# Attention block with a local convolution: key buffers of the last group, order of the first query stack, place of the local norms, and fetch of the softmax sums

## The chip, the cores and the metric

The kernel runs on one core of one Trainium2 chip. The metric is the device time of one execution in microseconds (us). The engines are named as in the profile: PE (TensorE, matrix products; PEld its weight loads), DVE (VectorE), ACT (ScalarE), POOL (GpSimd) and SP (SyncE, which here issues transfers only). Each works off its own instructions in the order in which the program gives them and waits for others by semaphores.

## The reference

For four images of 384 channels and 48 x 48 pixels (2304 tokens), in float32, eight heads of 48 channels:

```python
local = lax.conv_general_dilated(x, conv_w, window_strides=(1, 1), padding='SAME', feature_group_count=C)   # 7 x 7, one filter a channel
local = local * inv[None, :, None, None] + (bn_beta - bn_mean * inv)[None, :, None, None]
x_norm = _layernorm(x_flat, ln_gamma, ln_beta)
q, k, v = heads(x_norm @ qkv_w.T + qkv_b)
local_q = heads(_layernorm(local_flat, ln_gamma, ln_beta))
q = q + local_q
attn = softmax(einsum('bhnd,bhmd->bhnm', q, k) * scale)
out = einsum('bhnm,bhmd->bhnd', attn, v) @ proj_w.T + proj_b
out = x_flat + out
```

(`heads` stands for the reshape to eight heads; the rest is cut.)

## The kernel before

**Tiling.** Keys, values and projections go by six token groups of 384 columns (g = 0 to 5; `G`). Queries go by five groups of rows (8, 10, 10, 10, 10 rows: 384 or 480 columns), numbered t = 0 to 19 over the four images, so that t = 0, 5, 10, 15 begin an image. Heads are worked in four pairs.

**Stages.** First a prologue makes image 0's keys, values and queries group by group (the loop `for g in range(1, NG)` from L1063). Then, for each t, twelve slots follow: slot s takes head pair s // 3 and six of the eighteen key blocks of 128 tokens. In a slot `score_batch` has PE compute six blocks of scores (36 matmuls, L952), ACT takes the exponential of each block from PSUM into a `pt` buffer (L960), and `weigh_batch` has PE multiply the six blocks into the values (24 matmuls, L967) and ACT copy the sums out (L849, L859). Before t = 5, 10 and 15 stands a key stage (`"kv"`, L1112 and on) which makes the next image's keys and values and also projects and writes out the image before.

**PSUM.** All products use pairs of banks from one rotation of four (`two_banks`, L105): scores, sums, means, projections. A product whose pair is still to be read stops PE, and everything behind it.

**The convolution** runs on DVE: 147 taps (49 for each of three channel chunks) for each t, one instruction a tap (L305, L309), into `acc{t}`, which rotates through three buffers. A planner (`plan`, L398) spreads the taps over half slots and steps of the key stage, in proportion to the room that `spare` and `spare_at_keys` (L336, L364) say DVE has there, so that each `acc{t}` is done at its due point; `convolve("slot", t, s, half)` issues the taps of one point. In image 0's prologue `convolve_first(n)` issues fixed numbers.

**The local norm** of `acc{t+1}` (class `Norm`, L419) takes, in image 0, the means over channels with PE: a sum over chunks on DVE (`sum`, L451-452), the mean on PE (`mean_of_sum`, L478), `centre` on DVE (L489), squares on ACT (L446), their sum on DVE (`sum_squares`, L451-452 again) and mean on PE, `root` on ACT (Ln, Exp, Square: L497-499), `newton` on DVE (L505-506), then `local_end` (L797) and `query_end` (L806), which adds the result to the projected queries. These steps hang on slot numbers counted from `first`, 8 for t = 0 and 7 for t = 1 to 3; `early` is true for t = 0 to 3 of image 0 only. Later images move the sums over partitions through DRAM (`out`, `few_...`).

**The query stack** of a pair, `qs`, holds the high part (`high_queries`, ACT, L820), the low part (`low_queries`, DVE, L825) and copies of rows moved by six SP transfers (L830, L832). The first score of t waits for the stack of pair 0.

**The keys.** Projection u of group g gives a tile `k` in the rotation `pt` of four, high part by ACT (L658), low part by DVE (`low`, L661, called by `lows_out`). `keys_out` then issues the transfers that lay them out: for u = 0 on SP straight into the stack of pair 0 (`ks`, L591-594), for the others on POOL into DRAM (`wide`, L591-619). POOL also loads the later stacks (`load_keys`, L628) and the slabs of x.

**The sums.** `divide(t)` fetches the softmax sums from DRAM with an SP transfer (`rd`, L888), takes reciprocals on DVE (L889) and spreads them (`rb`). In the key stage it is called at group 1 (L1140). SP takes its transfers in order; one that waits holds those behind it.

Of the kernel before, what the change touches and what calls it, by code (L numbers as in the profile page):

```python
# [16 lines left out]
P = 128  # L17
NH = 8
# [29 lines left out]
def unshifted_pass(  # L48
# [287 lines left out]
    def spare(t, s, half):  # L336
        b, g = divmod(t, NA)
        first, second = norm_slots(t)
        time = 3.6 - (0.0 if half else 0.6) - (0.6 if half and s % 3 == 1 else 0.0)
        if b + 1 < B and g >= begins(b + 1):  # L340
            time -= {(2, 1): 2.3, (4, 1): 2.2, (5, 1): 2.3, (7, 0): 0.4, (8, 0): 2.6}.get(
                (s, half), 0.0
            )
        if g:
            time -= {(2, 0): 0.7, (7, 1): 1.4}.get((s, half), 0.0)
        if t + 1 < NA:
            time -= {(first + 1, 0): 1.4, (first + 2, 0): 4.3, (first + 3, 0): 0.6}.get(
                (s, half), 0.0
            )
        elif g < NA - 1:  # L350
            time -= {(3, 1): 2.3, (5, 1): 2.2, (6, 1): 2.3, (8, 0): 0.4, (9, 0): 4.5}.get(
                (s, half), 0.0
            )
        return max(0.3, time) * columns_of(t) / G
# [64 lines left out]
    class Norm:  # L419
# [73 lines left out]
        def root(self, at=None):  # L493
            at = slice(0, self.n) if at is None else at

            y, u = self.buf[:, 1, at], self.buf[:, 2, at]
            nc.scalar.activation(u, self.m[:, at], AF.Ln, bias=eps)  # L497
            nc.scalar.activation(y, u, AF.Exp, scale=-0.5)
            nc.scalar.activation(u, y, AF.Square, scale=0.5**0.5)

        def newton(self, at=None):
            at = slice(0, self.n) if at is None else at
# [127 lines left out]
    def from_x(b, g, before=None, ao=None):  # L630
# [22 lines left out]
        def key(u, r):  # L653
            project(r[:, :G], lambda c: w_qk[:, c, 1, u, :], lambda c: src[:, c, :])
            yield
            bias = qkb[:, 1, u : u + 1]
            k = work.tile([P, 2, GM], HALF, tag="pt", name=f"k{b}_{g}_{u}", bufs=4)[:, :, :G]
            nc.scalar.activation(k[:, 0, :], r[:, :G], AF.Identity, bias=bias)  # L658

            def low():  # L660
                nc.vector.scalar_tensor_tensor(  # L661
                    k[:, 1, :], r[:, :G], bias, k[:, 0, :], ALU.add, ALU.subtract
                )
                keys_out(b, g, u, k)

            lows.append(low)
            yield
# [210 lines left out]
                        out=ao[r + HD : r + 64, c, :], in_=ao3[r + 16 * c : r + 16 * c + 16]  # L878
                    )

    def divide(t):

        n = columns_of(t)
        few = NH * n // P
        rd = work.tile([P, NH * GM // P], F32, tag="rd", name="rd")[:, :few]
        rb = work.tile([P, CC, GM], F32, tag="rb", name="rb", bufs=1)[:, :, :n]
        rden = dram.tile([NH, n], F32, tag=f"rden{n}", name=f"rden{t}")
        nc.sync.dma_start(out=rd, in_=outputs[t][2].rearrange("h (k f) -> (h k) f", f=few))  # L888
        nc.vector.reciprocal(rd, rd)  # L889

        for bound, op in ((SAFE, ALU.is_le), (1 / SAFE, ALU.is_ge)):
# [47 lines left out]


    halves = [slice(64 * i, 64 * i + 64) for i in range(2)]
    jobs = deque()
    weighing = deque()

    def score(t, p, kb):
# [29 lines left out]
    def score_batch(t, s):  # L975
        p, k0 = s // (KB // BATCH), s % (KB // BATCH) * BATCH
        for kb in range(k0, k0 + BATCH):
            score(t, p, kb)

    def weigh_batch(t, s):  # L980
        p, i = s // (KB // BATCH), s % (KB // BATCH)
# [81 lines left out]
    for g in range(1, NG):  # L1063

        last = g == NG - 1
        making = from_x(0, g)
        both(making)
        assert not last or n_first >= each - PE_TAPS
        norm = Norm(accs[0] if last else xn[0, g + 1])
        norm.mean_by_chunk(norm.src)  # L1070
        if last:
            added = output_bias()
        if g in (3, 5):
            keep_stack(0, g // 2 - 1)
        convolve_first(8 if last else 7)
        norm.centre()
        norm.squares()
        both(making)
        if not last:
            convolve_first(6)  # L1080
            both(making)
        norm.mean_by_chunk(norm.buf)
        norm.root()
        if last:
            convolve_first(9)
        lows_out(1)
        if last:
            both(making)
        both(making)
        convolve_first(4 if last else 9)  # L1090
        if not last:
            lows_out(2)
        if last:
            local_end(0, norm.newton())
        else:
            norm.scale(norm.newton())
        next(making)
        if last:
            query_end(0)
            high_queries(0, 0)  # L1100
            low_queries(0, 0)
        next(making)
        if not last:
            convolve_first(7)
    lows_out(2)
    nc.vector.tensor_add(pb, pb, added)
    plan(n_first - (each - PE_TAPS))
# [2 lines left out]
    for t in range(NT):  # L1110
        b, g = divmod(t, NA)
        if g == 0 and b:  # L1112
# [4 lines left out]
            for gk in range(NG):  # L1117
# [6 lines left out]
                old = norms_x.get(gk - 1)  # L1124
                both(making)
                convolve("kv", t, gk, 0)
                if new is not None:
                    norms_x[gk] = Norm(xn[b, new])
                    norms_x[gk].sum()
                    norms_x[gk].out()  # L1130
# [6 lines left out]
                    old.few_variance()  # L1137
                    old.few_root()
                if gk == 1:
                    rb = divide(t - 1)  # L1140
                if gk == 5:
                    norm.few_variance()
                    norm.few_root()
# [7 lines left out]
                    high_queries(t, 0)  # L1151
                both(making)
                convolve("kv", t, gk, 2)
                lows_out(1)
                if new is not None:
                    norms_x[gk].few_centre()
                    norms_x[gk].squares()
                if gk == 4:
                    norm.few_centre()
                    norm.squares()  # L1160
                if gk == 5:
                    low_queries(t, 0)
                both(making)
                convolve("kv", t, gk, 3)
                lows_out(2)
# [17 lines left out]
        first, second = norm_slots(t)  # L1183
        for s in range(NSLOT):
            pair, part = divmod(s, KB // BATCH)
            if t == 0 and s == first + 3:
                high_queries(t + 1, 0)
            score_batch(t, s)
            if part == 0 and pair < NP - 1:
                high_queries(t, pair + 1)  # L1190
# [32 lines left out]
                norm_x.few_variance()  # L1223
            if following and s == second:
                norm.few_variance()
            if t == 0 and s == first + 3:
                low_queries(t + 1, 0)
            convolve("slot", t, s, 0)
            sums_add()
            if early and s == first:  # L1230
# [2 lines left out]
            if early and s == first + 1:  # L1233
                norm.centre()
                jobs.extend(norm.square_jobs())
            if early and s == first + (2 if t == 0 else 3):
                local_end(t + 1, norm.newton())
                query_end(t + 1)
            if coming and s == X_SLOTS[1]:
                norm_x.few_root()  # L1240
            if following and s == second:
                norm.few_root()
            weigh_batch(t, s)
            if early and s == first:
                norm.mean_of_sum()
            if t == 0 and s == first + 1:
                norm.mean_kept(norm.buf)
                norm.root()
            if t and early and s == first + 2:
                norm.mean_of_sum()  # L1250
                norm.root()
            if t and early and s == first + 3:
                high_queries(t + 1, 0)
            convolve("slot", t, s, 1)
            if part == 0 and pair < NP - 1:
                low_queries(t, pair + 1)
            if t and early and s == first + 1:
                norm.sum_squares()
            if t and early and s == first + 3:
                low_queries(t + 1, 0)  # L1260
            if following and s == second + 1:
                low_queries(t + 1, 0)
            if coming and s == X_SLOTS[0]:
# [580 lines left out]
```

## Time and profile before

| | us |
|---|---|
| median of 3 runs (2768.09 to 2769.07) | 2768.7 |
| profiled execution | 2768.89 |
| its span, first to last instruction | 2767.1 |
| idle of PE in the span (2767.1 - 2728.2) | 38.9 |
| one slot of 384 columns: scores 3.42, weighing 4.09, from one slot's start to the next | 7.38 |
| one slot of 480 columns: scores 4.17, weighing 5.05, from start to start | 9.08 |
| one tap on DVE, mean over all | 0.66 |
| one exponential on ACT, mean | 0.94 |

The granted TensorE clock was 0.996 on average. In lines of the profile an arrow `<-` stands between what is written and what is read; `x6` is a number of instructions; in timelines the first two numbers are the start and the length in us, and brackets hold the idle time of the engine before it and what ended it. `SPq` marks a transfer's issue by SyncE. In the list of waits the numbers are the total in us, how often, and the longest; in tables by stretches each engine has its busy time with the number of instructions, and after POOL come the granted clock, the share of the transfer engines, and GB/s.

### The profile page before, as it was taken

The page shows a single profiled execution, that of the slowest core. Times are in us where ns is not written, and L with a number is a line of the kernel's source. Part 1 is how long each engine was busy: PE and PEld are TensorE (multiplying, and loading weights), DVE is VectorE, ACT ScalarE, POOL GpSimd, SP SyncE. Part 2 cuts the span into 40 slices and gives each one's busy share as a digit, 9 for nine tenths or more (in the row PEclk, how much of TensorE's full clock was granted, in tenths as well). Part 3 has the DMA queues.
Part 4 walks back from the last instruction along what each step waited for, and adds up shares of the span by engine and source line. Part 5 has one row for each costly group of instructions (what it writes and reads, how often), then busy time and mean ns, then how long its engine had stood idle before and what let it go on. Part 6 is the DMA issues. An engine that isn't in the chain of part 4 may idle for free.

```text
span 2767.1 us, 46151 instructions
## 1 busy us (share of the span) xinstructions
PE 2728.2 (99%) x16374; PEld 1547.9 (56%) x16374; DVE 2354.3 (85%) x4114; ACT 1638.4 (59%) x2262; POOL 695.0 (25%) x1273
## 2 busy tenths in 40 slices
PE   9999999999999999999999999999999999999999
PEld 6565555555555655555555665555555565555555
DVE  7999999999898999989889899898788899986202
ACT  4356666676324766776622666767652276666662
POOL 5741101112375111010257310101126711110110
PEclk9999999999999999999999999999999999999999
DMA  7454544446356455454545554545635545444442
GB/s 141 97 141 124 130 121 123 125 133 182 87 152 156 116 147 129 123 146 120 158 129 143 159 143 120 131 131 140 148 109 159 145 128 133 138 135 128 145 146 72
DMA packets 163297, 369.14 MB, mean 133 GB/s; under 512 B 61488, under 2 KB 112208, under 8 KB 163056
## 3 DMA queue, kind: packets, MB, share of 16 engines
q0 software_dynamic: 76992, 284.75, 36.0%
q1 hardware_dynamic: 83072, 77.72, 12.5%
q10 hardware_dynamic: 2992, 3.62, 0.4%
q8 instruction: 132, 2.16, 0.3%
q14 instruction: 109, 0.89, 0.1%
HBM read 258.14 MB, written 64.14 MB: 116 GB/s over the span
## 4 chain that ended last, share of the span: by engine, by line
PE 83%; DVE 6%; DMA 5%; POOL 3%; issue 1%; SPq 1%; ACT 1%; DVEq 0%; ACTq 0%; POOLq 0%
PE o L967 40%; PE r L952 33%; PE r L568 9%; DVE acc L309 3%; DMA wide<-k 1%; POOL wide L594 1%; DMA qs<-qs 1%; DMA slab<-in_x_dram 1%; POOL wide L619 1%; DMA parts<-part 1%; DVE k L661 0%; POOL wide L592 0%; DVE xn L806 0%; DVE acc L797 0%; POOL wide L613 0%
## 5 line engine op out<-in xcount | busy, mean ns | idle before, releaser
L309 DVE SCALAR_TENSOR_TENSOR acc<-slab,vec,acc 128x470 f32<-128x470 f32 (+9 forms) x2871 | 1687.7, 662 | 1.2
L960 ACT ACTIVATE pt<-r 128x960 f32<-128x960 f32 (+1 forms) x1440 | 1249.2, 943 | 272.7 <-PE o L967 151.4
L967 PE MATMUL o<-pt,v 128*64 128x480 f32 (+1 forms) x5760 | 1166.2, 554 | 4.6 <-ACT pt L960 4.6
L952 PE MATMUL r<-qs,ks 64*128 64x480 f32 (+1 forms) x8640 | 976.7, 375 | 19.2 <-DMA qs<-qs 13.3
L952 PEld LDWEIGHTS r<-qs,ks 64*128 64x128 f32 x8640 | 790.6, 185 | 286.6 <-issue 178.1
L967 PEld LDWEIGHTS o<-pt,v 128*64 128x64 f32 x5760 | 392.1, 137 | 663.6 <-issue 570.3
L628 POOL DMA_DIRECT2D ks<-wide x228 | 165.7, 727 | 1353.3 <-PE r L952 1278.6
L568 PE MATMUL r<-xn,w_qk 128*128 128x384 f32 x864 | 283.7, 486 | 0.0
L849 ACT COPY o<-o 113x480 f32<-113x480 f32 (+1 forms) x160 | 87.1, 544 | 294.9 <-PE o L967 294.9
L568 PEld LDWEIGHTS r<-xn,w_qk 128*128 128x128 f32 x864 | 164.2, 190 | 114.5
L568 PE MATMUL r<-w_v,xn 128*128 128x384 f32 x432 | 145.0, 488 | 2.4 <-DVE xn L563 2.4
L868 DVE TENSOR_TENSOR ao<-ao,o 113x480 f32<-113x480 f32 (+1 forms) x120 | 76.2, 635 | 73.2 <-ACT o L849 73.0
L650 ACT COPY v<-r 128x384 f32<-128x384 f32 x72 | 32.1, 480 | 174.2 <-PE r L568 174.1
L568 PEld LDWEIGHTS r<-w_v,xn 128*128 128x128 f32 x432 | 81.3, 190 | 61.5 <-DVE xn L563 4.1
L594 POOL DMA_DIRECT2D wide<-k x192 | 96.9, 509 | 17.0 <-issue 10.0
L825 DVE TENSOR_TENSOR qs<-xn,qs 128x480 fp32r<-128x480 f32 (+1 forms) x60 | 38.2, 637 | 65.3 <-ACT qs L820 65.3
L619 POOL DMA_DIRECT2D wide<-k x192 | 92.7, 488 | 0.5 <-DMA wide<-k 0.5
L613 POOL DMA_DIRECT2D wide<-k x144 | 72.1, 504 | 64.5 <-ACT k L658 59.4
L568 PE MATMUL r<-af,w_o 128*128 128x384 f32 (+1 forms) x270 | 86.0, 471 | 1.5 <-DVE k L661 1.5
L113 POOL DMA_DIRECT2D slab<-in_x_dram x76 | 45.7, 608 | 149.1 <-DVE acc L309 148.6
L859 ACT COPY ao<-o 113x480 f32<-113x480 f32 (+1 forms) x60 | 32.7, 545 | 74.7 <-PE o L967 74.7
L868 DVE TENSOR_TENSOR aot<-aot,o 113x480 f32<-113x480 f32 (+1 forms) x40 | 25.6, 640 | 56.8 <-ACT o L849 56.6
(137 smaller groups left out, 1326.7 us busy)
## 6 DMA issues: line engine op xcount, KB each, us to landing
ks<-wide POOLq DMA_DIRECT2D x228, 768.0 KB, 5.3
qs<-qs SPq DMA_DIRECT2D x352, 60.0 KB
wide<-k POOLq DMA_DIRECT2D x480, 24.0 KB, 1.9
slab<-in_x_dram POOLq DMA_DIRECT2D x24, 432.0 KB, 7.9
wide<-k POOLq DMA_DIRECT2D x192, 48.0 KB, 1.8
wide<-ks POOLq DMA_DIRECT2D x12, 768.0 KB, 4.2
xr<-in_x_dram POOLq DMA_DIRECT2D x16, 576.0 KB, 6.2
rb<-rden SPq DMA_DIRECT2D x32, 270.0 KB
```

Of the source, the lines that this page charges most:

```text
L113: queue.dma_start(out=dst[p0 : p0 + piece.shape[0]], in_=piece)
L309: nc.vector.scalar_tensor_tensor(dst, src, weight, dst, ALU.mult, ALU.add)
L568: nc.tensor.matmul(dst, lhsT=weights(c), rhs=src(c), start=c == 0, stop=c == CC - 1)
L594: queue.dma_start(out=dst[r + 32 * i : r + 32 * i + 32, 1], in_=k[r + 16 : r + HD, 1])
L613: nc.gpsimd.dma_start(out=last[16 * u : 16 * u + 16, 0], in_=k[r : r + 16, 0])
L619: nc.gpsimd.dma_start(out=last[to : to + 16, 1], in_=k[r : r + 16, 1])
L628: nc.gpsimd.dma_start(out=place_keys(b, p, i), in_=wide[b, p][:, :, at])
L849: nc.scalar.copy(part[0 : 64 + HA], sums[0 : 64 + HA, 0, :n])
L868: nc.vector.tensor_add(dst, dst, part[0 : 64 + HA])
L952: nc.tensor.matmul(r[:, j, :n], lhsT=ks[rows, w, at], rhs=qs[rows, m, :], start=i == 0, stop=i == 2,)
L960: nc.scalar.activation(pt, r[:, :, :n], AF.Exp, scale=SCALE)
L967: nc.tensor.matmul(sums[halves[j], 0, : columns_of(t)], lhsT=values[t // NA, kb // NB][:, first : first + 64], rhs=pt[:, j, :], start=i == ...
```

## The change

1. Image 0's prologue, last group: the mean of `acc0` is taken at the end of group 4; squares, root, `local_end`, `query_end` and the first query stack come before the last projections' evictions, the first key projection's low part and its SP transfers after the stack's. The taps of that group are dealt out as 6, 9, 2, 4 instead of 8, 9, 4.
2. Key stage, group 5: `low_queries(t, 0)` stands before `lows_out(1)`.
3. The three `k` tiles of group 5 lie in buffers of `rb`, `acc` and `sq`, not in `pt`, in all images.
4. `divide` is split: the fetch of the sums (`sums_in`) is issued at group 0 of the key stage, the rest stays at group 1. The other callers fetch as before.
5. Local norms in image 0. For t = 0 the root's three steps go between the score blocks of the next slot (`between`), and the query stack of t + 1 is made in slot first + 2 instead of first + 3. For t = 1 to 3 the mean of squares and the root stand ahead of slot first + 2's weighing, `local_end` and `query_end` at the end of that slot, the stack in slot first + 3 ahead of its second half's taps.
6. `spare` has the DVE times of these steps at their new places, and for t = 1 to 3 two entries of 1.3 for the sums over chunks that it had not counted.

```diff
@@ -344,9 +344,18 @@
         if t + 1 < NA:
-            time -= {(first + 1, 0): 1.4, (first + 2, 0): 4.3, (first + 3, 0): 0.6}.get(
-                (s, half), 0.0
-            )
+            if t:
+                time -= {
+                    (first, 0): 1.3,
+                    (first + 1, 0): 1.4,
+                    (first + 1, 1): 1.3,
+                    (first + 2, 1): 4.3,
+                    (first + 3, 1): 0.6,
+                }.get((s, half), 0.0)
+            else:
+                time -= {(first + 1, 0): 1.4, (first + 2, 0): 4.3, (first + 2, 1): 0.6}.get(
+                    (s, half), 0.0
+                )
         elif g < NA - 1:
@@ -497,6 +506,12 @@
             nc.scalar.activation(u, y, AF.Square, scale=0.5**0.5)
+
+        def root_jobs(self):
+            y, u = self.buf[:, 1], self.buf[:, 2]
+            yield lambda: nc.scalar.activation(u, self.m, AF.Ln, bias=eps)
+            yield lambda: nc.scalar.activation(y, u, AF.Exp, scale=-0.5)
+            yield lambda: nc.scalar.activation(u, y, AF.Square, scale=0.5**0.5)
@@ -654,7 +669,12 @@
             bias = qkb[:, 1, u : u + 1]
-            k = work.tile([P, 2, GM], HALF, tag="pt", name=f"k{b}_{g}_{u}", bufs=4)[:, :, :G]
+            if g == NG - 1:
+                tag, bufs = (("rb", 1), ("acc", 3), ("sq", 2))[u]
+                k = work.tile([P, CC, GM], HALF, tag=tag, name=f"k{b}_{g}_{u}", bufs=bufs)
+                k = k[:, 0:2, :G]
+            else:
+                k = work.tile([P, 2, GM], HALF, tag="pt", name=f"k{b}_{g}_{u}", bufs=4)[:, :, :G]
             nc.scalar.activation(k[:, 0, :], r[:, :G], AF.Identity, bias=bias)
@@ -878,14 +898,19 @@
-    def divide(t):
+    def sums_in(t):
+        few = NH * columns_of(t) // P
+        rd = work.tile([P, NH * GM // P], F32, tag="rd", name="rd")[:, :few]
+        nc.sync.dma_start(out=rd, in_=outputs[t][2].rearrange("h (k f) -> (h k) f", f=few))
+        return rd
+
+    def divide(t, rd=None):
...
         few = NH * n // P
-        rd = work.tile([P, NH * GM // P], F32, tag="rd", name="rd")[:, :few]
+        rd = sums_in(t) if rd is None else rd
         rb = work.tile([P, CC, GM], F32, tag="rb", name="rb", bufs=1)[:, :, :n]
         rden = dram.tile([NH, n], F32, tag=f"rden{n}", name=f"rden{t}")
-        nc.sync.dma_start(out=rd, in_=outputs[t][2].rearrange("h (k f) -> (h k) f", f=few))
         nc.vector.reciprocal(rd, rd)
@@ -939,7 +964,7 @@
     halves = [slice(64 * i, 64 * i + 64) for i in range(2)]
-    jobs = deque()
+    jobs, between = deque(), deque()
     weighing = deque()
@@ -976,6 +1001,8 @@
             score(t, p, kb)
+            if between:
+                between.popleft()()
@@ -1065,16 +1092,18 @@
         both(making)
-        assert not last or n_first >= each - PE_TAPS
-        norm = Norm(accs[0] if last else xn[0, g + 1])
-        norm.mean_by_chunk(norm.src)
         if last:
             added = output_bias()
+        else:
+            norm = Norm(xn[0, g + 1])
+            norm.mean_by_chunk(norm.src)
+            convolve_first(7)
         if g in (3, 5):
             keep_stack(0, g // 2 - 1)
-        convolve_first(8 if last else 7)
         norm.centre()
         norm.squares()
+        if last:
+            convolve_first(6)
         both(making)
@@ -1083,25 +1112,28 @@
             convolve_first(9)
-        lows_out(1)
-        if last:
-            both(making)
-        both(making)
-        convolve_first(4 if last else 9)
-        if not last:
-            lows_out(2)
-        if last:
             local_end(0, norm.newton())
-        else:
-            norm.scale(norm.newton())
-        next(making)
-        if last:
             query_end(0)
             high_queries(0, 0)
+            both(making)
             low_queries(0, 0)
-        next(making)
-        if not last:
-            convolve_first(7)
+            convolve_first(2)
+            lows_out(1)
+            both(making)
+            convolve_first(4)
+            both(making)
+            continue
+        lows_out(1)
+        both(making)
+        convolve_first(9)
+        lows_out(2)
+        norm.scale(norm.newton())
+        both(making)
+        if g == NG - 2:
+            assert n_first >= each - PE_TAPS
+            norm = Norm(accs[0])
+            norm.mean_by_chunk(norm.src)
+        convolve_first(7)
     lows_out(2)
@@ -1124,6 +1156,8 @@
                 convolve("kv", t, gk, 0)
+                if gk == 0:
+                    rd = sums_in(t - 1)
                 if new is not None:
@@ -1137,7 +1171,7 @@
                 if gk == 1:
-                    rb = divide(t - 1)
+                    rb = divide(t - 1, rd)
                 if gk == 5:
@@ -1151,6 +1185,8 @@
                 convolve("kv", t, gk, 2)
+                if gk == 5:
+                    low_queries(t, 0)
                 lows_out(1)
@@ -1158,8 +1194,6 @@
                     norm.squares()
-                if gk == 5:
-                    low_queries(t, 0)
                 both(making)
@@ -1183,8 +1217,6 @@
             pair, part = divmod(s, KB // BATCH)
-            if t == 0 and s == first + 3:
-                high_queries(t + 1, 0)
             score_batch(t, s)
@@ -1223,8 +1255,6 @@
                 norm.few_variance()
-            if t == 0 and s == first + 3:
-                low_queries(t + 1, 0)
             convolve("slot", t, s, 0)
@@ -1233,31 +1263,36 @@
                 jobs.extend(norm.square_jobs())
-            if early and s == first + (2 if t == 0 else 3):
+            if t == 0 and s == first + 2:
                 local_end(t + 1, norm.newton())
                 query_end(t + 1)
+                high_queries(t + 1, 0)
+            if t and early and s == first + 3:
+                high_queries(t + 1, 0)
             if coming and s == X_SLOTS[1]:
...
                 norm.few_root()
+            if t and early and s == first + 2:
+                norm.mean_of_sum()
+                norm.root()
             weigh_batch(t, s)
...
                 norm.mean_kept(norm.buf)
-                norm.root()
+                between.extend(norm.root_jobs())
+                between.popleft()()
+            if early and s == first + (2 if t == 0 else 3):
+                low_queries(t + 1, 0)
+            convolve("slot", t, s, 1)
             if t and early and s == first + 2:
-                norm.mean_of_sum()
-                norm.root()
-            if t and early and s == first + 3:
-                high_queries(t + 1, 0)
-            convolve("slot", t, s, 1)
+                local_end(t + 1, norm.newton())
+                query_end(t + 1)
             if part == 0 and pair < NP - 1:
...
                 norm.sum_squares()
-            if t and early and s == first + 3:
-                low_queries(t + 1, 0)
             if following and s == second + 1:
...
```

## What was predicted

> **What bounds the kernel now.** First the page's busy table and the chain's shares by engine:
>
> ```profile
> PE 2728.2 (99%) x16374; PEld 1547.9 (56%) x16374; DVE 2354.3 (85%) x4114; ACT 1638.4 (59%) x2262; POOL 695.0 (25%) x1273
> ...
> PE 83%; DVE 6%; DMA 5%; POOL 3%; issue 1%; SPq 1%; ACT 1%; DVEq 0%; ACTq 0%; POOLq 0%
> ```
>
> TensorE (PE) is busy 2728 of 2767 us and no matmul is added or taken away, so at most PE's stalls can go. Second, the list of PE's waits:
>
> ```profile
> PE r L952 <- DMA qs<-qs: 13.3, 11, 2.5
> PE o L967 <- ACT pt L960: 4.6, 2, 2.7
> PE r L952 <- ACT pt L960: 3.2, 4, 1.1
> ...
> PE r L568 <- DVE xn L563: 2.4, 2, 1.9
> ...
> PE r L568 <- DVE k L661: 1.5, 2, 0.8
> ```
>
> In order of time these stand at the first scores of image 0 (162.9, 166.1), of query groups t=1 (264.2), 2 (379.6), 3 (493.2), 4 (606.5) and of images 1, 2, 3 (860.1, 1530.1, 2198.4); in the slots before t=1 to 4 (248.5, 362.1, 476.0, 589.1: ACT); in the key stage (758.6, 764.7, 2099.8); and at the first weighings of images 1 and 3 (866.8, 2205.8). Third, the table by stretches shows what a stall costs besides: after it, a stretch of 3.4 us at clock 0.50 (last column but two).
>
> ```profile
> 261.60:265.00 3.40, 1.05 (x9) 0.68 (x10) 3.40 (x6) 0.35 (x1) 0.00 (x0) 1.00 0.61 172
> 265.00:268.40 3.40, 3.40 (x20) 2.98 (x18) 3.40 (x7) 2.76 (x3) 0.00 (x0) 0.50 0.16 36
> ```
>
> It happens after 162.6, 265.0, 1531.4 and 2200.4: some 1.7 us each, since half the work of a full stretch is left over. Fourth, VectorE's (DVE's) busy time while image 0's queries run:
>
> ```profile
> 161.00:261.00 100.00, 94.49 (x728) 59.53 (x728) 95.46 (x158) 64.81 (x96) 27.50 (x48) 0.97 0.52 141
> 261.00:378.00 117.00, 113.93 (x729) 61.24 (x725) 114.89 (x188) 77.88 (x96) 13.74 (x21) 0.99 0.46 126
> 378.00:492.00 114.00, 112.08 (x726) 60.40 (x728) 112.25 (x184) 77.75 (x97) 13.97 (x21) 1.00 0.47 126
> ```
>
> DVE (third busy column) is as full as PE: 95.5 of 100, 114.9 of 117, 112.3 of 114 us. The reader is to see that a stall of PE removed there lets PE run ahead of DVE, and PE meets DVE again at the local norm.
>
> **The skill.** "TensorE: Matmul & The Clock Gate", "What's actually happening": the array's clock goes to half when little was done in a free-running window of 3413 ns. The trace agrees: its half-clock stretches begin whole multiples of 3.413 us apart (162.607, 265.007: thirty). "DMA: Bandwidth & Descriptors", "Issuing engines are not separate DMA queues": transfers of SyncE and GpSimd share the same engines. The trace agrees in the times of one and the same transfer: a qs row copy was back 2.2 us after its issue at 163.95 (PE went on at 166.11), and 5.0 after 259.08 (264.12), when POOL's next stack load, issued at 257.7, ran beside it.
>
> **Part 1, last keys in other buffers** (k of group 5: rb, acc, sq instead of pt), and **first stack's rest ahead of the keys' rows**, images 1 to 3. Six SP transfers of the query stack (0.64 us each) now stand behind eight of key rows:
>
> ```profile
> 850.85 1.21 SPq L594 DMA_DIRECT2D ks<-k  x2
> ...
> 854.76 0.64 SPq L830 DMA_DIRECT2D qs<-qs  x1
> ...
> 857.77 0.43 PE L952 MATMUL r<-qs,ks 64*128 64x384 f32 x1
> ...
> 860.10 0.62 PE L952 MATMUL r<-qs,ks 64*128 64x384 f32 x4 [1.89 <-DMA qs<-qs]
> ...
> 865.86 0.81 ACT L960 ACTIVATE pt<-r 128x768 f32<-128x768 f32 x1 [2.85 <-DMA wide<-k]
> ...
> 866.82 4.10 PE L967 MATMUL o<-pt,v 128*64 128x384 f32 x24 [2.72 <-ACT pt L960]
> ```
>
> Put first they start when DVE has subtracted, 850.2; the sixth starts 3.3 later and lands some 3.1 after (857.4 to 861.0 took that): 856.6, before PE comes at 857.8. The key rows move back 4 us to about 859; they serve slot 2, at 872, so nothing waits. The exps no longer wait for the POOL copies out of k. What is late next: PE's fourth score block reuses the PSUM pair that the last outputs held, freed when DVE ends L933 at 860.92 (DVE runs without a gap from 842.5 to there, whatever PE does). Block four would start at 859.5, so it waits 1.4; the remaining three blocks take 1.71, weighing starts at 862.7 instead of 866.8: 4.1 gained. By the same sum image 2 (L933 ends 1529.96; 1531.7 for 1535.5): 3.8; image 3 (2198.84; 2200.6 for 2205.8): 5.2. Sum 13.1. The acc, rb and sq buffers taken were last read long before (rb at 775.7, sq at 831), and their next users come slots later: nothing.
>
> **Part 2, sums fetched sooner.** In the key stage DVE stands 7.66 us (752.43) and 8.07 (2093.59) for rd, whose SP transfer is queued behind a four<-parts transfer. Fetched one group earlier it stands on SP after the aot copies (720.6) and costs the queue one issue, 0.6, which the 4.9 us until the part sums are used covers. DVE then does the key lows seven microseconds earlier, so PE's 0.85 and 1.95 (758.6, 764.7) and 0.68 (2099.8) go: 3.5. Image 2 has no PE stall there: nothing. Parts 1 and 2 for images 1 to 3: 16.6 us. DVE has idle time there to follow (2.7 at 870, 2.3 at 892, 5.7 at 978).
>
> **Part 3, image 0's start.** The mean of acc is taken a group earlier; DVE reaches Newton after 22 taps of 0.625 and the centring (1.3), 136.8 + 15.1 = 151.9, but the root on ACT ends about 152.2; then 4.3 to the end of query_end, low part at 157.1, SP's six transfers to 160.4 and 2.2 to land: 162.6 instead of 166.1. PE, done with the projections at about 160.6, still waits 2, then runs slot 0 in 7.4 instead of 9 us: it ends at 170.0 instead of 175.1. SP's key rows go out behind, for slot 2 at 185.
>
> **Part 4, the local norms of t=1 to 4.** Roots go among the exps (t=0) or ahead of the weighing (t=1 to 3); the query stack is made about half a slot sooner. By themselves: 248.5's 1.06 stays, because all three root steps still precede the third exp, whose PSUM pair the sums need; 264.2's 2.35 and its 1.7 of clock go; 3 x 0.7 and 1.22, 0.49, 0.75 go. With 5.1 of part 3 that would be 13.7.
>
> **But DVE must keep up.** It has been busy without a gap from 136.8 to 174.7, and its work before each norm is fixed. Old end of the channel sum (L452) and start of PE's mean (L478), with my estimate of the new end:
> - t=0: 232.44, 234.10. The plan's rule with the new rooms puts 101 taps instead of 99 ahead (+1.2), a wait of 1.44 for ACT goes, 0.5 for the root comes: 232.8. PE would be there at 229.3; it stands 3.5, and a stall like that has halved the clock, +1.7. Left: 1.3, after the halving -0.5.
> - t=1 begins about 3.6 earlier than before. Its sum: 336.72, 338.38. Taps ahead are equal; DVE's wait for the root is now 4.2 (it has only one tap to do there) against 2.96: new end 337.5. PE stands some 2.7; left 0.9, less another halving (even chance).
> - t=2: 451.47, 452.25. DVE's wait for the root in t=1, 2.5 or more, replaces 1.80; one tap more: new end 452 to 455. Left: -3 to 0.
> - t=3: 561.52, 565.31, slack 3.8 and 3.96 of DVE idle before it (546.0): no stall.
> From there 0.70, 0.49, 0.71, 0.75 are PE's for good. Image 0 in all: between 3 gained (no halvings) and 3 lost (three of them). I take 0: the 13.7 are used up by DVE.
>
> **Sum.** 2768.9 (profiled execution; span 2767.1, 1.8 around it; the median of the runs is 2768.7) - 16.6 - 0 = 2752.
>
> **Rivals.**
> A. DVE's work is looser than I count (taps shift among slots, PE's stalls fall in the norm's shadow): the 13.7 stay too, less a stall or so: 2769 - 16.6 - 12 = 2740. For it: new rooms give DVE less at the slots of the norms. Against: gap-free 80 us stretches.
> B. The key stage gives only half: stack transfers collide with POOL's (5 us to land instead of 3.1), block four's wait falls across a clock window (+1.7 each): 16.6 - 8 - 1 = 2761 with image 0 slightly worse.
> C. Slower. The mean of squares in slot first+2 now stands ahead of the weighing on PE's in-order queue; behind it wait 24 weighing matmuls, then ACT's sum copies and the next scores. I count sum_squares ending at 349.9, 1.4 before PE's mean at 351.3. If DVE falls six microseconds or more behind that, each of t=1 to 3 costs over 6 plus 1.7 of clock, 23 together, more than parts 1 and 2 bring: 2775. Against: DVE idles 4 in t=2.
>
> **Numbers.** My forecast 0.57 (its own range 2748 to 2757), A 0.20, B 0.14, C 0.06, and 0.03 for an end in between. 0.2%, 5.5 us, is about what a measurement here tells from no change: faster 0.89 (mine, A, and 0.12 of B), same 0.05, slower 0.06. Range 2740 to 2762: it holds mine, 0.12 of A and 0.11 of B, and leaves out 0.20.
>
> **What would show it.** Right: no wait on qs at images 1 to 3's first scores, the third exp free, a PE wait of 0.3 to 1.5 on L933's PSUM pair; no rd wait in the key stage; in image 0 new PE waits at L478 behind DVE L452 in t=0, 1 and 2, with half clock after some. Wrong: PE runs through those norms without waiting (then A), or waits at L478 for sum_squares (C), or qs still late at 857 (B).

## The result, and the profile after

Four runs of the changed kernel took 2743.26 to 2746.51 us, median 2746.05; four of the kernel before, on the same chip, had the median 2768.89. The ratio is 0.9911, with a 95% interval of 0.9894 to 0.9928, which is 20 to 29 us; the medians lie 22.8 us apart. The profiled execution took 2745.88 us with a span of 2744.1.

The page of the changed kernel, its busy table and the chain's shares by engine:

```profile
PE 2722.1 (99%) x16374; PEld 1545.0 (56%) x16374; DVE 2354.4 (86%) x4114; ACT 1639.0 (60%) x2262; POOL 697.5 (25%) x1273
...
PE 90%; DVE 8%; DMA 1%; ACT 1%; SPq 0%; issue 0%; POOL 0%; DVEq 0%; ACTq 0%; POOLq 0%
```

The span is 23.0 us shorter. PE's idle time fell from 38.9 to 22.0 (2744.1 - 2722.1): 16.9. Its busy time fell by 6.1 for the same matmuls. Some 3.8 of this is half clock: PE was busy for 20.0 us at half clock before and for 12.5 now, and half of such time is lost; 1.2 of the 3.8 lie in the prologue, in code that is the same. Another 1.9 lies in four slots of image 0, whose matmuls had been recorded as longer at full clock (see "What was mis-sized in image 0"). DVE works as long as before. In the chain, DMA and POOL fell from 5% and 3% to 1% and 0%, while DVE rose from 6% to 8%. The list of PE's waits says where the changed kernel still waits:

```profile
PE r L487 <- DVE sq L461: 5.2, 3, 3.6
PE r L977 <- DMA qs<-qs: 4.6, 5, 1.6
...
PE r L977 <- DMA ks<-k: 1.0, 1, 1.0
PE r L977 <- DVE xr L958: 0.9, 2, 0.7
PE o L992 <- ACT pt L985: 0.4, 1, 0.4
PE r L977 <- ACT pt L985: 0.4, 1, 0.4
```

(Lines moved: scores L952 to L977, weighing L967 to L992, the mean L478 to L487, the channel sum L452 to L461, Newton L505 to L520, the output sum L933 to L958.) The wait for `qs` fell from 13.3 to 4.6, all but 0.4 of it in image 0, that of the weighing from 4.6 to 0.4; those of the key stage on DVE's `k` are gone. (The 1.0 under `ks<-k`, at 160.40, is a wait for the query stack too: by their semaphores the stack's sixth copy landed at 160.26, and the key copies issued at 158.41 and 159.10 were complete only after 160.40.) New is the first line: PE's mean over channels stands behind DVE's channel sum, in t = 0, 1 and 2. The new waits for the output sum, 0.66 and 0.26, are the PSUM pair that was to be late next.

The start of image 1's first slot, in the timeline of the changed kernel:

```profile
848.75 2.52 PE L977 MATMUL r<-qs,ks 64*128 64x384 f32 x24
...
849.61 2.92 ACT L985 ACTIVATE pt<-r 128x768 f32<-128x768 f32 x4 [5.00 <-DMA wide<-k]
...
851.92 1.32 PE L977 MATMUL r<-qs,ks 64*128 64x384 f32 x12 [0.66 <-DVE xr L958]
...
853.17 4.09 PE L992 MATMUL o<-pt,v 128*64 128x384 f32 x24
```

From first score to weighing it now takes 853.17 - 848.75 = 4.4 us; before it was 866.82 - 857.77 = 9.05.

Where the time went, from the starts of slots in both profiled executions (us against the kernel before; a second execution of the changed kernel, `changed_again` below, beside it):

| from ... to | changed | again | predicted |
|---|---|---|---|
| prologue, up to code that is the same in both | -2.3 | -0.5 | 0 |
| rest of prologue, t = 0 to 2, up to slot 9 of t = 2 | +1.1 | 0.0 | |
| from there to slot 1 of t = 4 | -4.5 | -4.6 | |
| image 0 without the first row | -3.4 | -4.6 | 0 |
| key stage and first slot, image 1 | -8.0 | -8.0 | -6.9 |
| image 2 | -4.1 | -4.6 | -3.8 |
| image 3 | -5.2 | -6.0 | -5.9 |

The first row is no gain of the change but luck: it lies ahead of all changed code, and over all profiled kernels that stretch came out anywhere from 2.3 us shorter to 1.6 longer.

### The profile page after: what moved, and what is told of

It is laid out like the page before. It is cut to its first block, busy times and chain, and to the rows that moved or that the text cites. A ratio compares the mean times of both kernels' runs of the same rounds, so it can differ in the third digit from the quotient of the medians.

```text
span 2744.1 us, 46096 instructions
## 1 busy us (share of the span) xinstructions
PE 2722.1 (99%) x16374; PEld 1545.0 (56%) x16374; DVE 2354.4 (86%) x4114; ACT 1639.0 (60%) x2262; POOL 697.5 (25%) x1273
## 4 chain that ended last, share of the span: by engine, by line
PE 90%; DVE 8%; DMA 1%; ACT 1%; SPq 0%; issue 0%; POOL 0%; DVEq 0%; ACTq 0%; POOLq 0%
PE o L992 38%; PE r L977 31%; PE r L583 19%; DVE acc L309 6%; DMA qs<-qs 1%; DVE xn L826 0%; DVE acc L817 0%; PE r L487 0%; DVE qs L845 0%; SPq L852 0%; DVE xr L958 0%; DVE k L681 0%; PE r L324 0%; PE r L1037 0%; DVE ao L888 0%
## 5 line engine op out<-in xcount | busy, mean ns | idle before, releaser
L992 PE MATMUL o<-pt,v 128*64 128x480 f32 (+1 forms) x5760 | 1166.2, 554 | 0.4 <-ACT pt L985 0.4
L977 PE MATMUL r<-qs,ks 64*128 64x480 f32 (+1 forms) x8640 | 971.6, 374 | 7.0 <-DMA qs<-qs 4.6
L977 PEld LDWEIGHTS r<-qs,ks 64*128 64x128 f32 x8640 | 787.1, 185 | 273.6 <-issue 173.7
L992 PEld LDWEIGHTS o<-pt,v 128*64 128x64 f32 x5760 | 392.4, 137 | 660.0 <-issue 567.5
L609 POOL DMA_DIRECT2D wide<-k x192 | 97.2, 510 | 16.6 <-issue 10.0
L695 ACT ACTIVATE xn<-r,qkb 128x384 f32<-128x384 f32 x72 | 41.2, 580 | 63.4 <-PE r L583 61.8
```

The lines of the kernel that those rows point to most:

```text
L609: queue.dma_start(out=dst[r + 32 * i : r + 32 * i + 32, 1], in_=k[r + 16 : r + HD, 1])
L977: nc.tensor.matmul(r[:, j, :n], lhsT=ks[rows, w, at], rhs=qs[rows, m, :], start=i == 0, stop=i == 2,)
L992: nc.tensor.matmul(sums[halves[j], 0, : columns_of(t)], lhsT=values[t // NA, kb // NB][:, first : first + 64], rhs=pt[:, j, :], start=i == ...
```

## Experiments

Each ratio is against the kernel before on the same chip: a median of 2771.3 us (17 runs) for the first four of the table, 2772.1 (27 runs) for the last four.

| kernel | median us (runs) | ratio to before, 95% |
|---|---|---|
| image 0's part alone | 2769.64 (13) | 0.9993 [0.9985, 1.0002] |
| keys' part alone | 2749.98 (5) | 0.9924 [0.9911, 0.9938] |
| changed, fewer taps | 2737.31 (4) | 0.9878 [0.9863, 0.9893] |
| changed, room for Newton moved | 2739.82 (4) | 0.9885 [0.9870, 0.9901] |
| row order alone | 2772.67 (13) | 1.0002 [0.9994, 1.0010] |
| buffers alone | 2764.96 (14) | 0.9976 [0.9966, 0.9986] |
| Newton moved, second stack sooner | 2741.29 (4) | 0.9890 [0.9876, 0.9905] |
| changed, again | 2745.60 (4) | 0.9909 [0.9894, 0.9923] |

### Which half of the change brings the time

Image 0's part alone: items 1, 5 and 6, with the keys as before.

```diff
-            if g == NG - 1:
-                tag, bufs = (("rb", 1), ("acc", 3), ("sq", 2))[u]
...
+            k = work.tile([P, 2, GM], HALF, tag="pt", name=f"k{b}_{g}_{u}", bufs=4)[:, :, :G]
...
-                if gk == 0:
-                    rd = sums_in(t - 1)
...
-                    rb = divide(t - 1, rd)
+                    rb = divide(t - 1)
```

(`low_queries(t, 0)` also stands behind `lows_out(1)` again.)

> The image 0 parts of the change alone (prologue order, local norms, rooms of the planner); keys in pt, key rows first and the sums fetched late as before. Theory (DVE is as full as PE in image 0): PE meets DVE at the channel sums of t=0, 1, 2 whatever it gained before, so image 0 gives 2 to 5 us and the later images nothing: 2764 to 2767. Even the loss of a free pt buffer in image 0's first slot does not show in the end, because DVE decides. Rival (PE's stalls simply add up): 13.7 us, 2755.

The median is 1.7 us below the kernel before, and the interval reaches from 4.2 faster to 0.6 slower: no gain can be told from nothing, and the rival's 13.7 is out. The trace has the waits of PE's mean on DVE that the changed kernel has, 1.41 in t = 1 and 3.55 in t = 2:

```profile
PE r L487 <- DVE sq L461: 5.0, 2, 3.6
```

It also has one of 3.99 at 167.80: scores that wait for an exponential, which starts only at 166.94, when a transfer has ended. By the program its `pt` buffer holds `k` until the copies out of it are done. In the changed kernel, where that `k` lies elsewhere, the wait isn't there, so image 0's start needs the buffers of item 3 as well. Without them the first slot takes 17.08 us, in the changed kernel 11.48. With the prologue's difference taken off, this execution is therefore 5.6 behind the changed kernel at slot 1 of t = 0, but only 2.3 behind at slot 1 of t = 4, where it is 1.1 ahead of the kernel before: most of what was lost at the start didn't count in the end.

Keys' part alone: items 2, 3 and 4 put into the kernel before.

> The other three parts alone: last keys in other buffers, query stack ahead of the key rows in the key stages, sums fetched sooner; image 0 in the order of before. Theory: 2.8 + 4.1 in image 1, 3.8 in image 2, 0.7 + 5.2 in image 3, 16.6 in all and nothing in image 0: 2752. The two parts should add up to the whole change (22.8). Rival (transfers of POOL and SP collide, half of it): 2761.

Measured 21.3 us below the kernel before on that chip. In the trace it gains 17.3 us from slot 1 of t = 4 to slot 1 of image 3, as much as the whole change did there. (The trace of the kernel before is of an execution of 2768.9 us, one of its faster ones: its 17 runs here lie between 2767.5 and 2775.8. So the medians lie further apart than the traces.) Image 0's part differs by -1.7 and the keys' by -21.3, together -23.0; the whole change gave -22.8 in its own comparison and -26.5 in that of `changed_again`. The halves add up as far as these runs can tell, and that is to some 4 us.

Item 4 was not run alone. But in image 1's key stage the keys' part gains 3.3 us, as the whole change does, while the three kernels without item 4 gain 0.7 (image 0's part) and 0.0 (row order alone, below) or lose 1.2 (buffers alone, below). So those 3.3 are put down to item 4.

### The two edits of the keys, one by one

Row order alone is item 2, one call moved:

```diff
                 convolve("kv", t, gk, 2)
+                if gk == 5:
+                    low_queries(t, 0)
                 lows_out(1)
...
-                if gk == 5:
-                    low_queries(t, 0)
```

> Kernel before with one edit: in the key stage the query stack's low part and its SP transfers stand ahead of the key rows. Theory: two waits end at nearly the same moment at an image's start, the stack's rows (860 to 861) and the exps' buffer, which POOL's copies out of k hold (third exp at 865.9, 1533.9, 2204.9 in the kernel before). With the first gone alone, weighing still starts after the third exp: nothing in images 1 and 3, 0.6 in image 2: 0 to 2 us faster, the clock stretches making it uncertain. Rival (each edit brings its share of the 13.1): 6 to 7 us.

Buffers alone is item 3:

```diff
-            k = work.tile([P, 2, GM], HALF, tag="pt", name=f"k{b}_{g}_{u}", bufs=4)[:, :, :G]
+            if g == NG - 1:
+                tag, bufs = (("rb", 1), ("acc", 3), ("sq", 2))[u]
+                k = work.tile([P, CC, GM], HALF, tag=tag, name=f"k{b}_{g}_{u}", bufs=bufs)
+                k = k[:, 0:2, :G]
+            else:
+                k = work.tile([P, 2, GM], HALF, tag="pt", name=f"k{b}_{g}_{u}", bufs=4)[:, :, :G]
```

> Kernel before with one edit: the last group's k in other buffers, key rows still first. Theory: the stack's rows still land at 861, five blocks of scores follow (3.0 at full clock, 4.6 at half), so weighing starts at 864.1 instead of 866.8, at 1535.6 as before, at 2204.0 instead of 2205.8: 4.5 us faster, so that with the other edit alone (0.6) the sum is 5, and the two together 13. Rival (each brings its share): 6 to 7 us.

Timeline of the kernel with the row order alone, PE and ACT at image 2's first slot:

```profile
1530.23 3.42 PE L952 MATMUL r<-qs,ks 64*128 64x384 f32 x30
...
1534.54 0.81 ACT L960 ACTIVATE pt<-r 128x768 f32<-128x768 f32 x1 [2.64 <-DMA out_dram<-xr]
...
1535.41 0.79 PE L952 MATMUL r<-qs,ks 64*128 64x384 f32 x6 [1.76 <-ACT pt L960]
...
1537.74 0.81 ACT L960 ACTIVATE pt<-r 128x768 f32<-128x768 f32 x1 [2.38 <-DMA wide<-k]
...
1538.69 6.73 PE L967 MATMUL o<-pt,v 128*64 128x384 f32 x24 [2.50 <-ACT pt L960]
```

The wait for `qs` is gone, and thirty scores run at once. Then the exponentials come to `pt` buffers that hold `k` until POOL has copied it (`DMA wide<-k` releases ACT; for the one at 1534.54 the profile names another transfer). PE stands 1.76 and 2.50, the clock halves (the weighing takes 6.73 us instead of 4.09), and from first score to weighing it is 8.46 us; in the kernel before it was 7.50 (1528.04 to 1535.54). In images 1 and 3 it is 1.6 less than before, which half clock in the weighing takes back: over the three first slots the trace is 4.2 us longer (0.6, 3.6 and 0.0). In the median nothing is gained, at the low end of what was expected.

Timeline of the kernel with the buffers alone, image 1's first slot:

```profile
857.12 1.33 SPq L837 DMA_DIRECT2D qs<-qs  x2
...
857.51 0.44 PE L957 MATMUL r<-qs,ks 64*128 64x384 f32 x1
...
859.70 0.62 PE L957 MATMUL r<-qs,ks 64*128 64x384 f32 x4 [1.76 <-DMA qs<-qs]
...
860.68 3.04 PE L957 MATMUL r<-qs,ks 64*128 64x384 f32 x31 [0.36 <-issue]
...
861.13 2.92 ACT L965 ACTIVATE pt<-r 128x768 f32<-128x768 f32 x4 [7.76 <-PE r L957]
```

Here four exponentials run in a row, and the wait for `qs`, whose last transfers go out at 857.1, is what is left. Its median is 7.1 us below the kernel before, where 4.5 was expected; this number alone would fit the rival's 6 to 7 as well. In the trace the first slots of images 1, 2 and 3 gain 2.9, 0.5 and 3.5; in image 3, where I had counted 1.8, no half clock followed. What settles it is the sum: the first slots gain 6.9 by the buffers alone and nothing by the row order alone, and in the keys' part, where both are made, 13.4 (4.6, 3.6 and 5.1). Each edit alone runs into the wait that the other takes away.

### Does DVE set the time in image 0?

Four of the 49 taps of each chunk are left out in t = 1 to 4 (12 instructions a group), so that DVE has some 8 us less to do for each of these; the convolution is incomplete there.

```diff
             src, dst = part
+            if t in (1, 2, 3, 4) and tap in taps[-4:]:
+                yield
+                continue
```

> The changed kernel with 4 of the 49 taps left out for t=1 to 4 of image 0 (12 DVE instructions each, about 7.4 us; the outputs of those rows lack these taps). Theory: PE's waits for the channel sums (0.2, 1.4 and 3.6 us) and the half clock after the last vanish, and a part of the query stack waits (1.2, 0.6): 6 to 10 us faster than the changed kernel, 2736 to 2740. If DVE is not what holds PE there: 2746, as the changed kernel.

All three waits of the mean on DVE are gone, and no half clock follows. PE's work is that of the changed kernel, and the time is some 9 us below it (0.0033 or 0.0031 of 2770, by its two ratios). So DVE is what holds PE back in image 0, as expected.

The second kernel of this question leaves DVE's work whole and moves it. The planner had taken 4.3 us for Newton and the ends out of the half slot before the root comes back, so DVE stood idle for the root; now that room is taken out of the next half slot.

```diff
-                    (first + 2, 1): 4.3,
+                    (first + 3, 0): 4.3,
...
-                time -= {(first + 1, 0): 1.4, (first + 2, 0): 4.3, (first + 2, 1): 0.6}.get(
+                time -= {(first + 1, 0): 1.4, (first + 2, 0): 1.5, (first + 2, 1): 3.4}.get(
```

> The changed kernel with rooms in the planner moved: for t=1 to 3 the 4.3 us stand at (first+3, 0) instead of (first+2, 1), for t=0 1.5 at (first+2, 0) and 3.4 at (first+2, 1) instead of 4.3 and 0.6, so that taps run while DVE waits for the root (2.5, 3.0, 4.7, 5.0 us idle in the changed kernel). Same instructions. Theory: DVE comes to t=2's channel sum about 4.2 us sooner, PE's waits there and at t=1 shrink to under 1 us and the half clock goes: 2740. If DVE's idle time there is not what PE pays later: 2746.

DVE's timeline around the root of t = 2, first in the changed kernel:

```profile
466.31 0.71 DVE L309 SCALAR_TENSOR_TENSOR acc<-slab,vec,acc 128x470 f32<-128x470 f32 x1
471.72 0.72 DVE L520 SCALAR_TENSOR_TENSOR sq<-sq,eps 128x480 f32<-128x480 f32 x1 [4.70 <-ACT sq L508]
```

and with the room moved:

```profile
462.85 4.89 DVE L309 SCALAR_TENSOR_TENSOR acc<-slab,vec,acc 128x470 f32<-128x470 f32 x8
467.65 0.71 DVE L520 SCALAR_TENSOR_TENSOR sq<-sq,eps 128x480 f32<-128x480 f32 x1
```

The 4.70 us in which DVE stood for ACT are filled by seven more taps. In this kernel's list of PE's waits the mean is left with one of 1.06, and it is no longer followed by half clock:

```profile
PE r L487 <- DVE sq L461: 1.1, 1, 1.1
```

Its median of 2739.8 us is the lowest of the kernels that do all the work, and what was expected. Its interval against the kernel before just overlaps the changed kernel's (0.9901 and 0.9894), so the 6 us between them rest on the single runs, 2737.9 to 2741.0 against 2743.3 to 2747.4, and on the traces.

### A transfer that came late in image 0

The changed kernel has a wait that I hadn't foreseen. Its timeline in slots 1 to 3 of t = 0:

```profile
173.49 0.76 POOL L638 DMA_DIRECT2D wide<-ks  x1
...
174.09 1.49 POOL L643 DMA_DIRECT2D ks<-wide  x2
...
174.98 2.20 SPq L852 DMA_DIRECT2D qs<-qs  x2
...
180.03 0.72 POOL L643 DMA_DIRECT2D ks<-wide  x1 [4.46 <-PE r L977]
...
186.10 3.05 PE L977 MATMUL r<-qs,ks 64*128 64x384 f32 x31 [1.63 <-DMA qs<-qs]
```

The last `qs` transfer of the second stack, issued at 176.6 and 48 KB long, is back only at 186.0, 9.4 us later; beside it run four moves of 768 KB that POOL issues from 173.5 on. To see what it costs, one kernel makes the stack's low part, and so its transfers, ahead of the taps of that half slot, on top of the moved room:

```diff
+            if t == s == 0:
+                low_queries(0, 1)
             convolve("slot", t, s, 1)
...
-            if part == 0 and pair < NP - 1:
+            if part == 0 and pair < NP - 1 and (t or s):
                 low_queries(t, pair + 1)
```

> The kernel with the taps ahead of Newton (newton_later) and one more edit: in slot 0 of t=0 the low part of pair 1's query stack and its six SP transfers stand ahead of the second half's taps instead of behind them. Theory: the last of these transfers no longer runs beside POOL's stack loads (issued at 176.6 in the changed kernel, back at 186.0), so the wait of 1.9 us at slot 3's first scores goes; part of it comes back at t=2's channel sum, where DVE still holds PE for 1.1: 1 to 2 us faster than newton_later. If the transfer is not starved but late by itself, or DVE takes all of it back: no difference.

The wait in slot 3 went, and in its place PE stood 2.61 at the mean of t = 0. The time didn't fall (2741.3 against 2739.8): the second of the two outcomes that had been named. `changed_again`, the changed kernel itself, says the same without an edit:

> The changed kernel itself beside the others, for a comparison on one chip: 22.8 us faster than before, and PE's waits for DVE L461 at L487 in t=0, 1 and 2 again (0.2, 1.4, 3.6 us), since they follow from DVE's work and not from the chip or the clock windows.

Here the medians lie 26.5 us apart (interval of the ratio 0.9894 to 0.9923), and the three waits of the mean are there again, though not in the sizes expected: 1.86, 1.15 and 2.92.

```profile
PE r L487 <- DVE sq L461: 5.9, 3, 2.9
```

The transfer landed at 186.1, almost the same moment as before, but PE came 1.7 us later in this execution and lost only 0.5 in the slot; it then stood 1.86 at the mean of t = 0 instead of 0.24. With the prologue's difference taken off its start, the mean begins at nearly the same moment in each of them:

| kernel | wait in slot 3 | wait at the mean | start of the mean | the same, prologue taken off |
|---|---|---|---|---|
| changed | 1.63 | 0.24 | 230.29 | 232.5 |
| changed again | none listed | 1.86 | 232.02 | 232.5 |
| Newton moved | 1.93 | none listed | 231.88 | 232.5 |
| the same, stack sooner | none | 2.61 | 234.42 | 232.8 |

In each of them the channel sum of DVE ends 0.15 us before. So the mean begins when DVE is there, whatever PE waited for earlier, and that wait of 1.6 us is free.

## Why the prediction was right, and which terms were off

**The bound.** PE, with only its stalls to win: right. 16.9 us less idle time and 6.1 us less busy time, more than half of it half clock, make up the 23.0.

**How near it came.** The measured 2746 is 6 us below the forecast of 2752 and just outside the range of 2748 to 2757 given for it; it is as far above rival A's 2740. The time alone would not tell the two apart. PE's waits at the mean do, and the experiments on DVE. Of the 6 us, 2.3 are luck in the prologue.

**Part 1 and 2, images 1 to 3.** 16.6 us predicted, 17.3 measured in the first execution, 18.6 in the second. Image 1 gave 4.6 from first score to the second slot and 3.3 in the key stage (4.1 and 2.8 predicted), image 2 4.1 (3.8), image 3 5.2 (5.9). What was late next was the pair held by the output sum in images 1 and 3, 0.66 and 0.26 us instead of 1.4; image 2 didn't wait for it. DVE's two waits of 7.66 and 8.07 for `rd` in the key stage are gone. The 13.1 for the first slots was the sum for both edits together (13.4 measured); that each hides the other's gain was not in the prediction, and only the experiments show it. Rival B (half of it) fell with the keys' part alone.

**Image 0: DVE takes it back.** The mechanism is shown: with 12 taps a group taken from DVE the three waits at the mean vanish and some 9 us more are gained; with its idle time filled one of 1.06 is left and some 6 are gained; image 0's part alone brings next to nothing. Rival A, in which the norms run through, fell; so did C: PE has no wait at the mean of squares in t = 1 to 3.

**What was mis-sized in image 0** is the net of 0, between 3 gained and 3 lost: it gave 3.4 and 4.6 in two executions. Two terms account for most of it.

First, "0.70, 0.49, 0.71, 0.75 are PE's for good", 2.65 in all, measured 4.5. I had taken these waits from the list of gaps. In the kernel before, a slot of t = 2 with such a wait looked like this:

```profile
472.39 2.88 PE L952 MATMUL r<-qs,ks 64*128 64x480 f32 x24
...
475.98 1.78 PE L952 MATMUL r<-qs,ks 64*128 64x480 f32 x12 [0.70 <-ACT pt L960]
...
477.70 5.05 PE L967 MATMUL o<-pt,v 128*64 128x480 f32 x24
```

and in the changed kernel:

```profile
471.26 4.18 PE L977 MATMUL r<-qs,ks 64*128 64x480 f32 x36
...
475.37 5.05 PE L992 MATMUL o<-pt,v 128*64 128x480 f32 x24
```

From first score to weighing it is 5.31 against 4.11: 1.20, not 0.70. The rest stood in the record as matmuls that took longer (12 in 1.78, where an undisturbed twelve take a third of 4.18, 1.39). The four slots were 10.29, 10.03, 10.28 and 10.27 us long and are 9.09, 9.09, 9.08 and 9.06.

Second, DVE's wait for the root in t = 0, predicted as 4.2, was 2.52; the 1.7 of half clock counted behind the mean, which would have put off the mean of squares and the root, didn't come (that link is worked out, no run isolates it). So the channel sum of t = 1 ended at 332.75, which is 335.0 with the prologue's 2.3 added, and not at 337.5. In t = 0 DVE ended where predicted (232.4 for 232.8), but PE stood 0.24 and 1.86 instead of 3.5, since slot 0 brought 3.9 and 4.0 instead of 5.1. PE went on there at 160.40 (162.7 with the prologue's 2.3; predicted 162.6), but slot 1 began 8.5 us later and not 7.4: a stretch at half clock, 160.59 to 164.01, had not been counted. Slot 3 took 2.0 more in the first execution. The sum of t = 2 ended at 450.6, a little ahead of the predicted 452 to 455, and PE stood there all the same. A half clock did come behind it, in the table by stretches of the changed kernel:

```profile
444.00:447.30 3.30, 0.90 (x6) 0.07 (x2) 3.30 (x7) 0.56 (x1) 1.28 (x3) 1.00 1.02 204
447.30:450.70 3.40, 2.20 (x4) 0.84 (x6) 3.37 (x6) 0.23 (x1) 0.00 (x0) 0.50 0.99 250
450.70:454.10 3.40, 3.40 (x18) 2.78 (x18) 3.40 (x6) 2.17 (x3) 1.35 (x2) 0.50 0.45 151
```

PE (first busy column) stands 3.60 for DVE (third, full), and two stretches run at 0.50. In `changed_again` the wait was 2.92 and only one stretch was halved; in the kernel with the room moved it was 1.06 and none was. The Trainium skill, "TensorE: Matmul & The Clock Gate", "What's actually happening", gives the length of the windows as 3413 ns, and this agrees: the halved stretches in the traces' clock record are 3.41 us long (in the changed kernel 160.59 to 164.01) or twice that (447.31 to 454.14).

**"248.5's 1.06 stays"** was nearly right: it became two waits of 0.40. The waits for the stack at 264.2 and 379.6, which Part 4 counted as gone, stayed in part: 1.17 and 0.56, in the second execution 1.46 and 1.25. They lie ahead of a mean at which PE waits for DVE anyway, so they are among what DVE takes back.

**A transfer misread.** The prediction has a `qs` copy back 2.2 us after its issue at 163.95. By the trace's chain and its semaphores it was the fourth copy of the stack, issued at 162.64, that let PE go at 166.11: 3.4 us. The copy of 259.08 is the fourth of its stack too, so 3.4 and 5.0 are the pair to compare (48 and 60 KB long); it is the same finding with a smaller difference. That Part 3, which used the 2.2, still had the stack's landing right (162.6 for 162.7) is partly luck.

**The distance in sum.** The prediction's sum, 2768.9 - 16.6, is 6.4 above the profiled 2745.9: 3.4 from image 0, 2.3 from the untouched prologue, 0.7 from images 1 to 3.

## What to carry to other kernels

Two waits that end near each other, here one behind SP's queue and one behind a buffer's release, must be taken away together; tried singly, one edit looked worthless here and the other half as good as the pair. Where a second engine is as full as the first, price a removed stall by when the second engine arrives, and look for the idle time of that second engine: a planner that leaves room for a step before the step's input is there leaves that room empty. And read a stall from the length of its slot against an undisturbed slot, since part of it can be recorded as slower instructions.

## What the runs showed of the hardware

**A small transfer beside large ones.** One `qs` copy of 48 or 60 KB took 3.4 us from issue to landing beside POOL's copies of `k` (issued at 162.64 in the kernel before), 5.0 beside one 768 KB load (259.08), and in the changed kernel 9.4 beside four 768 KB moves (176.58). In the second execution of that program the last one took 7.6 (178.46 to 186.07), so this delay isn't fixed. The Trainium skill, "DMA: Bandwidth & Descriptors", "Issuing engines are not separate DMA queues", says that such transfers share engines, which fits; what sets the length of the delay no run here explains.

**When half clock follows.** Each trace can be cut into windows of 3.413 us at the moments where its clock changes. Over all ten traces, without their first 30 and last 40 us, each full-clock window in which PE was idle, by its records, for 1.89 us or more was followed by a halved one, and none in which it was idle for 1.55 or less. In between both happened: 1.56 (from 2196.95) was followed by half clock in the kernel before, 1.85 (from 2203.78) was not. After a halved window came another one where PE was idle for 0.64 or more in it, and full clock where for 0.39 or less. So one wait can be dear or cheap by where it falls: the 3.60 of t = 2 put 2.4 into one window and 1.2 into the next, and two were halved; the 2.92 of `changed_again` put 2.7 and 0.3, and only one was.

**Scatter.** The first 36 us are the same code in all ten kernels, and their executions scatter there by up to 4 us (2.3 shorter to 1.6 longer than in the kernel before). The half-clock stretches differ: in the kernel before one ran from 9.0 to 15.8, in the changed kernel from 10.4 to 13.8, and in the keys' part, 0.7 shorter, there was none. They don't account for all of it; the waits there differ too, and the cause stays open. A gain of that size in one trace says nothing; the slots have to be compared one against another.
